# States of the recurrence handed to attention layer 0 in halves of four sequences, and a different order for one stretch of the norms

## The chip, the cores and the metric

The kernel runs on one core of a Trainium2 chip. The metric is device time in microseconds (us) for one execution. Five engines work side by side, each through its own queue in order: TensorE (PE, matmuls; its weight loads are listed as PEld), VectorE (DVE), ScalarE (ACT), GpSimd (POOL) and SyncE (SP, which issues nearly all DMAs). An instruction that waits holds up everything behind it on its engine.

## The reference

The input x has 8 sequences of 512 positions with 128 features. Two blocks follow each other.

```
xb = einsum('bsd,ed->sbe', layernorm(x), B)        # block 1
h  = tanh(h @ A.T + xb_t);  y_t = h @ C.T          # 512 steps in sequence, 8 sequences at once
x  = x + layernorm'(y + layernorm(x)) * gamma + beta
z  = layernorm(x)                                  # block 2: six layers
for i in range(6):
    z = attn(shift(z), Wqkv[i], ...) + z           # 16 heads of 64, window of 32, l2-normed q and k, rotary
    z = ffn(shift(z), W1[i], W2[i], ...) + z       # gated gelu, 341 hidden
out = x + z
```

`shift` takes the second half of the features from the position before. A token of layer 0 needs the state h of its own position, and through the window those of the 32 positions before. Nothing in layer 0 needs a later position, so attention of layer 0 can begin on early positions while the recurrence still runs.

## The kernel before

**The order is written out by hand.** The program is recorded in a manual schedule: each engine executes its instructions in the order in which the Python code emits them. There is no planner; what decides is where a call stands in the code.

**Chunks, parts, groups.** The 512 positions are cut into four chunks of 128. Layer 0's attention works on parts (c, h): chunk c, half h, a half being four sequences. The order of parts is (0,0) (0,1) (1,0) (1,1) (2,0) (3,0) (2,1) (3,1) (line 926). Each part makes two groups, one for each four of the eight pairs of heads, so group n belongs to part n // 2. Layers 1 to 5 have 16 groups each as well, 96 in all.

**Slots.** The main loop (line 1085) runs over n, and inside over t = 0..3. One `slot(n, t)` (line 956) mixes the work of four groups: scores and softmax of group n for 128 query rows (`scores`, `turn`, `less_max`, `exps`, `average`, `divide`, `turn_back`), the norms of group n+1 at t = 0 and 1 (`sums`, `solve`, `spread`, `finish`), the projections of group n+2 at t = 2 and 3 (`unit_a` makes `rawa`, `unit_b` makes `rawb`), and the output projection of group n-1 at t = 1 (`project` makes `yo`, then `add`). Five lists `fill[0]` to `fill[4]` hold what `run(0)` to `run(4)` emit between these.

**Norms.** `sums` adds squares on PE (`nsq`, line 430); `solve` makes inverse roots on DVE; `spread` broadcasts them on PE (`bc`, line 465), one PSUM bank for each of four units; `finish(c)` multiplies unit c with its `bc` on DVE (line 565) and sends it to qT or kbuf by four DMAs. Groups with n < 9 (`NREC`) have a pool of three PSUM banks for `rawa`, `rawb`, `nsq`, `bc`, `vps`, `yo`; later ones have four. In `slot(n, 1)` with n < 9, `spread` is emitted for units 0, 1, 2, then `finish(0)`, `less_max`, `spread` for unit 3, `exps`, `mask`, `finish(1)`, `average`, `finish(2)`, `finish(3)`, `project`, `divide`, `add`.

**Steps of the recurrence.** `Recurrence.step` (line 262) is one matmul `xb` of 128x8 on PE (line 281; two records, since fp32 goes in two passes) and one tanh `hT` on ACT (line 289); the next step's matmul waits for that tanh. Steps enter the stream in two ways. `tick(us)` is called after pieces of PE work with an estimate of their length and emits a step when 0.35 us have gathered. `alone()` (line 356) emits a step and two `warm` matmuls (line 361) that write nothing of use. The first chunk's 128 steps run by `alone()` before any group.

**From states to tokens.** After step 127 of a chunk, `queue(c)` (line 315) makes a list of 21 pieces: two `output` (PE: `yp`, line 302; DVE adds, line 311), the norm of all eight sequences (four `stats` pieces of two sequences, one `rsqrt` of 11 small DVE instructions, two `normalise` of four sequences), two `scale`, one `add` with a store of x1, the second norm in the same form, and two `turn` (PE transposes `rt_c`, ACT copies into xT). `output` sets `held` while steps may not go on. `run(k)` pops one piece at a time, in slots with t = 1 only outside `run(4)` and none that needs a PSUM bank except at `run(0)`.

**Who waits.** `begin(n)` calls `rec.need(c)` (line 377) before the first group of a part on chunk c. It emits `alone()` until the chunk is over and then all 21 pieces in one go, until both halves are posted. Ahead of the first group the loop of lines 1077 to 1081 pops the first chunk's pieces with an `alone()` after each from the third on. `need` is called at the head of a slot, so everything that the slot emits stands behind it on every engine.

Of the kernel before, what the change touches and what calls it, by code (L numbers as in the profile page):

```python
# [48 lines left out]
def mk_seq_preln_kernel(  # L49
# [102 lines left out]
    with tc.tile_pool(name="qk", bufs=2) as qkp, tc.tile_pool(  # L152
# [16 lines left out]
        class Recurrence:  # L169
# [19 lines left out]
            def stats(self, src, nm, bs=range(B)):  # L189
                if bs[0] == 0:  # L190
# [7 lines left out]
            def rsqrt(self, nm):  # L198
                x_, y, a = (
                    small.tile([P, B], F32, tag=f"r{i}", name=f"{i}_{nm}", bufs=1)  # L200
                    for i in "xya"
                )
                nc.vector.tensor_scalar_add(x_, self.mv[:, :, 1], EPS)
# [7 lines left out]
                self.rs = y  # L211
# [103 lines left out]
            def queue(self, c):  # L315
# [9 lines left out]
                def add():  # L325
                    nc.vector.tensor_add(x1, x1, o)
                    nc.sync.dma_start(x1_d[:, c], x1)

                def turn(q):
                    tp = self.turned(o, f"c{c}", q)  # L330
                    sq = slice(4 * q, 4 * q + 4)
                    nc.scalar.copy(xT[:, sq, c * P : (c + 1) * P], tp)
                    nc.scalar.copy(self.edge[D // 2 :, sq, c], tp[D // 2 :, :, P - 1])
                    if q:
                        self.posted = c + 1

                def norm(dst, src, nm):
                    for b in range(0, B, 2):
                        yield lambda b=b: self.stats(src, nm, (b, b + 1)), False
                    yield lambda: self.rsqrt(nm), False  # L340
                    for b in range(0, B, 4):
                        yield lambda b=b: self.normalise(dst, src, range(b, b + 4)), False


                self.pieces = [(lambda q=q: self.output(c, o, q), True) for q in range(2)]
                self.pieces += norm(o, o, f"b{c}")
                self.pieces += [(lambda: scale(slice(0, 4)), False)]
                self.pieces += [(lambda: scale(slice(4, 8)), False), (add, False)]
                self.pieces += norm(o, x1, f"c{c}")
                self.pieces += [(lambda q=q: turn(q), True) for q in range(2)]  # L350

# [25 lines left out]
            def need(self, c):  # L377

                while self.posted <= c:
                    if self.pieces:  # L380
                        self.piece()
                    else:
                        self.alone()
# [36 lines left out]
        class Norms:  # L420
# [3 lines left out]
            def __init__(self, sqs, which, op, floor, nm, inside):  # L424

                nsq = mm(f"nsq_{nm}")
                for half in range(len(sqs[0])):
# [10 lines left out]
                    rec.tick(0.93)  # L438
# [496 lines left out]
        def begin(n):  # L935
# [3 lines left out]
            if l == 0:  # L939
                c, h = b  # L940
                if g == 0:
                    rec.need(c)
# [13 lines left out]
        def slot(n, t, feed=None):  # L956
# [10 lines left out]
            back, bt = (cur, t - 2) if t > 1 else (old, NT - 2 + t)  # L967
            fill = [[] for _ in range(5)]
# [9 lines left out]
            if one and t == 1:  # L978
                fill[1] = [lambda: one.spread(range(4)), lambda: one.finish(0)]
                if n < NREC:  # L980

                    fill[1] = [lambda: one.spread((0, 1, 2)), lambda: one.finish(0)]
                    fill[2] = [lambda: one.spread((3,))]
# [36 lines left out]
            if feed and t == 2:  # L1020
                feed.apply()
            if cur:
# [12 lines left out]
            if one and t == 1:  # L1035
                one.finish(1)
            if last:
                last.average(lt)
            if one and t == 1 and not feed:
# [20 lines left out]
        with tc.manual_schedule():  # L1060
# [16 lines left out]
            for _ in range(2):  # L1077
                rec.piece()
            while rec.posted == 0:
                rec.piece()  # L1080
                rec.alone()
# [3 lines left out]
            for n in range(-1, len(todo) + 1):  # L1085
                m, l = n % GL, n // GL
                if n == NREC:
                    rec.need(NT - 1)
# [144 lines left out]
```

## Time and profile before

| | us |
|---|---|
| median of 3 runs (lowest, highest) | 3875.51 (3870.49, 3880.85) |
| profiled execution | 3878.7 |
| its span, first to last instruction | 3876.6 |
| first step of the recurrence to the last | 19.6 to 598.4 |
| scores of group 9, t = 0 (the first without the recurrence's pool) | 660.2 |

All that the change touches lies in the first 660 us of the span. "Busy" is the time in which an engine has an instruction running; the granted clock of PE is 1.00 at full speed and 0.50 at half. A row of the timeline gives the start, the duration of the rows merged in it, engine, line, operation and tile, and in brackets how long the engine was idle ahead of it and what it waited for.

Start of the scores (line 627) of each slot in us, read from PE's timeline:

| n | t=0 | t=1 | t=2 | t=3 |
|---|---|---|---|---|
| 0 | 176.6 | 183.5 | 193.6 | 202.7 |
| 1 | 214.1 | 223.2 | 238.9 | 246.8 |
| 2 | 292.6 | 301.8 | 317.5 | 325.4 |
| 3 | 336.8 | 345.9 | 361.6 | 370.4 |
| 4 | 381.7 | 391.0 | 406.6 | 414.6 |
| 5 | 425.9 | 438.8 | 456.8 | 469.2 |
| 6 | 496.6 | 505.8 | 521.6 | 529.5 |
| 7 | 541.7 | 550.9 | 566.6 | 574.5 |
| 8 | 625.8 | 632.2 | 644.9 | 651.1 |
| 9 | 660.2 | 667.0 | 675.8 | 682.2 |

### The profile page before, as it was taken

What the parts mean: (1) busy time and instruction counts of PE and PEld (TensorE: products, weight loads), DVE (VectorE), ACT (ScalarE), POOL (GpSimd) and SP (SyncE); (2) the same over time, 40 slices, a digit from 0 to 9 for tenths busy, and PEclk for the clock granted to TensorE, in tenths of its full rate; (3) what the DMA queues carried; (4) which work ended last, traced back from release to release, by engine and by line L of the source; (5) the groups of instructions that cost most, each with busy time, mean ns of one, the idle gap of its engine ahead of it and who ended that gap; (6) DMA issues with size and microseconds to landing.
All of it is one profiled execution on the core that took longest, in us unless ns stands there. A gap on an engine that the chain in (4) does not pass through costs nothing.

```text
span 3876.6 us, 159331 instructions
## 1 busy us (share of the span) xinstructions
PE 3553.3 (92%) x70178; PEld 2141.7 (55%) x70180; DVE 2542.5 (66%) x5208; ACT 1932.1 (50%) x3864; POOL 1827.0 (47%) x780
## 2 busy tenths in 40 slices
PE   8879897899999999999999999999999999999997
PEld 4556664545555555555555555555555555555553
DVE  3555655767677677677677677677677677677673
ACT  2344443545455455455455455455455455455452
POOL 0333332536365365355355355355355355365450
PEclk9889888999999999999999999999999999999998
DMA  3233443545345355355255354355354355354342
GB/s 124 64 82 86 97 100 86 121 94 128 77 111 116 69 125 126 77 115 114 67 127 125 74 117 113 72 128 120 73 117 110 75 130 120 77 117 111 73 110 60
DMA packets 366078, 390.54 MB, mean 101 GB/s; under 512 B 96846, under 2 KB 262220, under 8 KB 365260
## 3 DMA queue, kind: packets, MB, share of 16 engines
q1 hardware_dynamic: 364380, 378.09, 42.7%
q8 instruction: 553, 9.06, 1.1%
q10 hardware_dynamic: 1008, 2.27, 0.2%
q14 instruction: 137, 1.12, 0.1%
HBM read 34.56 MB, written 14.20 MB: 13 GB/s over the span
## 4 chain that ended last, share of the span: by engine, by line
PE 67%; DVE 20%; ACT 7%; issue 4%; DMA 1%; SPq 0%; DVEq 0%; ACTq 0%
PE sc L627 6%; PE rawb L538 5%; PE vps L587 5%; PE tp L656 4%; PE yo L712 4%; PE rawa L526 4%; DVE t L565 4%; PE nsq L430 4%; PE at L703 3%; PE fa L883 3%; DVE t L516 3%; PE xb L281 3%; PE yf L909 3%; PE fg L887 3%; DVE e L643 3%
## 5 line engine op out<-in xcount | busy, mean ns | idle before, releaser
L548 POOL TENSOR_TENSOR u<-rope_sb,bs 128x1024 f32<-128x1024 f32 x320 | 767.5, 2398 | 1349.7 <-ACT bs L544 1171.9
L549 POOL TENSOR_TENSOR t<-t,u 128x1024 f32<-128x1024 f32 x320 | 756.5, 2364 | 25.1
L565 DVE TENSOR_TENSOR t<-t,bc 128x1024 f32<-128x1024 f32 x320 | 376.1, 1213 | 287.2 <-PE bc L465 287.1
L516 DVE SCALAR_TENSOR_TENSOR t<-rawa,par_sb,rope_sb 128x1024 f32<-128x1024 f32 x320 | 409.4, 1279 | 204.4 <-ACT sq L530 199.0
L650 ACT ACTIVATE e<-e 128x512 f32<-128x512 f32 x320 | 201.8, 631 | 433.2 <-DVE e L643 319.4
L661 ACT COPY eT<-tp 128x512 f32<-128x512 f32 x320 | 187.4, 586 | 452.6 <-PE tp L656 452.6
L627 PEld LDWEIGHTS sc<-kbuf,qT 64*32 64x32 f32 x20480 | 226.5, 105 | 257.0 <-ACT sc L617 161.5
L627 PE MATMUL sc<-kbuf,qT 64*32 64x64 f32 x20480 | 280.1, 225 | 85.1 <-ACT sc L617 83.9
L538 PE MATMUL rawb<-xbuf,wqk 128*128 128x512 f32 x640 | 344.0, 619 | 0.0
L587 PE MATMUL vps<-wv,xbuf 128*64 128x256 f32 x2560 | 331.4, 391 | 0.0
L526 PE MATMUL rawa<-xbuf,wqk 128*128 128x512 f32 x640 | 328.3, 594 | 1.7 <-DVE t L516 1.7
L712 PE MATMUL yo<-aoT,wo 128*128 128x512 f32 x640 | 297.7, 608 | 33.4 <-DVE t L565 32.5
L674 PEld LDWEIGHTS av<-vbuf,eT 64*32 64x32 f32 x20480 | 227.2, 105 | 182.6 <-ACT sq L542 110.7
L674 PE MATMUL av<-vbuf,eT 64*32 64x65 f32 x20480 | 284.4, 225 | 14.5 <-issue 11.2
L692 DVE TENSOR_TENSOR ao<-av,rc 128x256 f32<-128x256 f32 x640 | 271.4, 424 | 21.9
L530 ACT ACTIVATE sq<-rawa 128x512 f32<-128x512 f32 x320 | 190.1, 594 | 153.5 <-PE rawa L526 153.5
L281 PEld LDWEIGHTS xb<-hT,s1w 128*128 128x128 f32 x1022 | 169.4, 198 | 174.2 <-ACT hT L289 118.4
L656 PE MATMUL tp<-ident,e 128*128 128x128 f32 x1280 | 205.9, 283 | 43.1 <-DVE rc L691 42.5
L587 PEld LDWEIGHTS vps<-wv,xbuf 128*64 128x64 f32 x2560 | 162.9, 137 | 140.1 <-issue 66.8
L643 DVE TENSOR_TENSOR e<-sc,mx 128x512 f32<-128x512 f32 x320 | 221.3, 692 | 27.5 <-PE rawa L526 0.5
L289 ACT ACTIVATE hT<-xb 128x8 f32<-128x8 f32 x512 | 91.5, 179 | 293.9 <-PE xb L281 279.6
L617 ACT CAST sc<-mask_sb 128x512 f32<-128x512 bf16 x384 | 227.7, 593 | 0.0
(282 smaller groups left out, 6264.3 us busy)
## 6 DMA issues: line engine op xcount, KB each, us to landing
qT<-t SPq DMA_DIRECT2D x640, 128.0 KB
kbuf<-t SPq DMA_DIRECT2D x640, 128.0 KB
vbuf<-vbuf SPq DMA_DIRECT2D x544, 130.0 KB
vbuf<-vbuf SPq DMA_DIRECT2D x160, 97.5 KB
xbuf<-xT SPq DMA_DIRECT2D x95, 128.0 KB
xbuf<-xT SPq DMA_DIRECT2D x80, 127.8 KB
wqk<-in_w_qkv SPq DMA_DIRECT2D x12, 512.0 KB
xf<-xT SPq DMA_DIRECT2D x24, 256.0 KB
```

What stands on the lines that cost most here:

```text
L516: nc.vector.scalar_tensor_tensor(t, self.twice(raw), scale, self.rope(isk, 1), ALU.mult, ALU.mult)
L526: nc.tensor.matmul(raw, self.wqk[:, c, 0], self.xs[:, WINDOW:], start=True, stop=True)
L538: nc.tensor.matmul(raw, self.wqk[:, c, 1], self.xs[:, WINDOW:], start=True, stop=True)
L548: nc.gpsimd.tensor_mul(self.wide(u), self.rope(isk, 0), self.twice(bs))
L549: nc.gpsimd.tensor_add(self.ts[c], self.ts[c], u)
L565: nc.vector.tensor_mul(t, t, self.bcs[c].unsqueeze(1).to_broadcast([P, 2, S]))
L587: nc.tensor.matmul(ps[par * KB : (par + 1) * KB, j], self.xs[:, k0 : k0 + KB], self.wv[:, par * GP * DH : (par + 1) * GP * DH], start=True ...
L627: nc.tensor.matmul(self.sc[blk * QB : (blk + 1) * QB, par, i, :], self.qT[rows, i, q0 : q0 + QB], kT[rows, i, :], start=False, stop=True, ...
L643: nc.vector.tensor_sub(self.e.rearrange("p i a k -> p a i k"), self.sc, mx.unsqueeze(3).to_broadcast([P, 2, GP, KB]),)
L656: nc.tensor.transpose(tp[:, i, :], self.e[:, i].rearrange("p a k -> p (a k)"), ident)
L674: nc.tensor.matmul(av[blk * QB : (blk + 1) * QB, i, :VW], self.eT[rows, i, blk * QB : (blk + 1) * QB], self.v[rows, BT * t + blk, i, :], s ...
L712: nc.tensor.matmul(self.yp, wo[:, self.g * GP + c, :], self.aoT[:, c, :], start=(c == 0), stop=(c == GP - 1),)
```

## The change

It has four parts, all in the phase of the recurrence.

1. `queue` makes 24 pieces instead of 21: both `output`, then for each half its own first norm (two `stats`, one `rsqrt` over four sequences, one `normalise`), `scale`, `add` with a store of half of x1, second norm and `turn`. `posted` counts halves, and `need(c, h)` waits for half h alone.
2. While `need` pops pieces it now emits one `alone()` step after each, unless steps are held or over.
3. `Norms` calls `tick` four times over its matmuls where it was called twice.
4. In `slot(n, 1)` with n < 9, `spread` is emitted for units 0 and 1 with `finish(0)` and `finish(1)` ahead of `less_max`, and for units 2 and 3 in `run(4)`, behind `project` and `divide` and ahead of `add`, with `finish(2)` and `finish(3)`; `average` moves ahead of `less_max`.

```diff
+            def rsqrt(self, nm, bs=slice(0, B)):
...
-                def add():
-                    nc.vector.tensor_add(x1, x1, o)
-                    nc.sync.dma_start(x1_d[:, c], x1)
+                def add(bs):
+                    nc.vector.tensor_add(x1[:, bs], x1[:, bs], o[:, bs])
+                    nc.sync.dma_start(x1_d[:, c, bs], x1[:, bs])
...
-                    if q:
-                        self.posted = c + 1
+                    self.posted = 2 * c + q + 1
...
+                self.pieces += [(lambda q=q: self.output(c, o, q), True) for q in range(2)]
+                for q in range(2):
+                    bs = slice(4 * q, 4 * q + 4)
+                    self.pieces += norm(o, o, f"b{c}{q}", bs)
+                    self.pieces += [(lambda bs=bs: scale(bs), False)]
+                    self.pieces += [(lambda bs=bs: add(bs), False)]
+                    self.pieces += norm(o, x1, f"c{c}{q}", bs)
+                    self.pieces += [(lambda q=q: turn(q), True)]
...
-            def need(self, c):
-
-                while self.posted <= c:
-                    if self.pieces:
-                        self.piece()
-                    else:
+            def need(self, c, h):
+
+                while self.posted <= 2 * c + h:
+                    self.piece()
+                    if self.t < S and not self.held:
                         self.alone()
...
-                    rec.tick(0.93)
+                        if m % 2:
+                            rec.tick(0.47)
...
-                    rec.need(c)
+                    rec.need(c, h)
...
+            tight = n < NREC
...
-                if n < NREC:
-
-                    fill[1] = [lambda: one.spread((0, 1, 2)), lambda: one.finish(0)]
-                    fill[2] = [lambda: one.spread((3,))]
+                if tight:
+                    fill[1] = [lambda: one.spread((0, 1)), lambda: one.finish(0)]
+                    fill[1] += [lambda: one.finish(1)]
+                    fill[4] = [lambda: one.spread((2, 3)), lambda: one.finish(2)]
+                    fill[4] += [lambda: one.finish(3)]
...
+            if tight and t == 1 and last:
+                last.average(lt)
             if cur:
                 cur.less_max(t)
...
-            if one and t == 1:
+            if one and t == 1 and not tight:
                 one.finish(1)
-            if last:
+            if last and not (tight and t == 1):
                 last.average(lt)
-            if one and t == 1 and not feed:
+            if one and t == 1 and not feed and not tight:
                 one.finish(2)
                 one.finish(3)
```

More of the change, by code (lines that the diff above doesn't have):

```diff
@@ L189, in stats @@
             def stats(self, src, nm, bs=range(B)):
-                if bs[0] == 0:
+                if bs[0] == 0 or bs[0] == 4 and len(bs) == 2:
                     self.mv = small.tile([P, B, 2], F32, tag="mv", name=f"mv_{nm}", bufs=1)
@@ L196, in stats @@
                     nc.vector.bn_aggr(mv[:, b, :], st)
[L198 to L201, printed above, removed]
+            def rsqrt(self, nm, bs=slice(0, B)):
+                self.rs = small.tile([P, B], F32, tag="ry", name=f"y_{nm}", bufs=1)
+                y = self.rs[:, bs]
+                x_, a = (
+                    small.tile([P, B], F32, tag=f"r{i}", name=f"{i}_{nm}", bufs=1)[:, bs]
+                    for i in "xa"
                 )
-                nc.vector.tensor_scalar_add(x_, self.mv[:, :, 1], EPS)
+                nc.vector.tensor_scalar_add(x_, self.mv[:, bs, 1], EPS)
                 nc.vector.tensor_scalar(
@@ L210, in rsqrt @@
                     nc.vector.scalar_tensor_tensor(y, a, 1.5, y, ALU.add, ALU.mult)
-                self.rs = y
             def normalise(self, dst, src, bs=range(B)):
@@ L333, in turn, with norm @@
                     nc.scalar.copy(self.edge[D // 2 :, sq, c], tp[D // 2 :, :, P - 1])
-                    if q:
-                        self.posted = c + 1
-                def norm(dst, src, nm):
-                    for b in range(0, B, 2):
+                    self.posted = 2 * c + q + 1
+                def norm(dst, src, nm, bs):
+                    for b in range(bs.start, bs.stop, 2):
                         yield lambda b=b: self.stats(src, nm, (b, b + 1)), False
[L340 to L350, printed above, removed]
+                    yield lambda: self.rsqrt(nm, bs), False
+                    yield lambda: self.normalise(dst, src, range(bs.start, bs.stop)), False
+                self.pieces += [(lambda q=q: self.output(c, o, q), True) for q in range(2)]
[6 more added lines that the diff above has]
+                    self.pieces += [(lambda q=q: turn(q), True)]
             def piece(self, bank=True):
@@ L1076, in mk_seq_preln_kernel @@
                 rec.alone()
[L1077 to L1081, printed above, removed]
+            rec.need(0, 0)
             for t in (2, 3):
@@ L1087, in mk_seq_preln_kernel @@
                 if n == NREC:
-                    rec.need(NT - 1)
+                    rec.need(NT - 1, 1)
                     recs.close()
```

## The prediction, made before the changed kernel ran

> **What bounds the kernel now.** I read the page's first lines, then the waits of PE in the phase of the recurrence, then PE, ACT and DVE over one slot, then stretches with their granted clock.
>
> ```profile
> span 3876.6 us, 159331 instructions
> PE 3553.3 (92%) x70178; PEld 2141.7 (55%) x70180; DVE 2542.5 (66%) x5208; ACT 1932.1 (50%) x3864; POOL 1827.0 (47%) x780
> ```
>
> PE is the bound. From group 9 on (660 us) the changed program keeps every engine's order, so only the first 660 us can move. PE's waits from 130 to 660 us (total, times, longest):
>
> ```profile
> PE rt_c L228 <- issue: 36.4, 2, 18.2
> PE xb L281 <- ACT hT L289: 11.0, 12, 5.4
> ...
> PE bc_c1h L465 <- DVE t_c1h L565: 4.2, 4, 1.1
> PE bc_c0h L465 <- DVE t_c0h L565: 4.0, 4, 1.1
> ```
>
> Two waits of 18.2 us are the flushes of all pieces for chunks 1 and 3. The `bc` waits are `spread(3)`, which needs the bank that `finish(0)` frees. What such a short wait costs is seen in slot (3,1), PE:
>
> ```profile
> 348.35 1.17 PE L465 MATMUL bc_c1h<-k_c1h,selt_sb 32*128 32x128 f32 x24
> 349.45 0.39 PE L281 MATMUL xb<-hT,s1w 128*128 128x8 f32 x2
> 350.89 1.35 PE L465 MATMUL bc_c1h<-k_c1h,selt_sb 32*128 32x128 f32 x8 [1.05 <-DVE t_c1h L565]
> ...
> 353.74 2.06 PE L712 MATMUL yo_c0h<-aoT_c0h,wo 128*128 128x512 f32 x2
> ...
> 359.34 1.10 PE L712 MATMUL yo_c0h<-aoT_c0h,wo 128*128 128x512 f32 x2
> 360.43 1.10 PE L526 MATMUL rawa_c1h<-xbuf,wqk 128*128 128x512 f32 x2
> ```
>
> The same `yo` takes 2.06 and then 1.10. The granted clock says why (stretch: length, PE busy, clock, DMA share, GB/s):
>
> ```profile
> 349.49:350.89 1.40, 0.35 (x6) 1.00 0.05 12
> 350.89:351.86 0.97, 0.97 (x8) 0.93 0.00 0
> 351.86:358.66 6.80, 6.80 (x77) 0.51 0.84 188
> ```
>
> An idle of 1.05 us is followed by 6.8 us at half clock, a loss of 3.4 us; together 4.45. This happens in all eight slots (0,1) to (7,1). In (8,1), without steps, an idle of 1.37 us brought only about 3.4 us at half. The Trainium skill ("TensorE: Matmul & The Clock Gate", section "HAM oscillation — how this bites in real kernels") tells one to avoid PE gaps above about 3.4 us. By that rule gaps of 1 to 2 us cost only themselves. The rows above disagree, and they decide. ACT and DVE in the same slot:
>
> ```profile
> 352.25 0.63 ACT L650 ACTIVATE e_c0h<-e_c0h 128x512 f32<-128x512 f32 x1 [2.20 <-DVE e_c0h L643]
> 352.79 0.58 ACT L617 CAST sc<-mask_sb 128x512 f32<-128x512 bf16 x1
> 353.92 0.18 ACT L289 ACTIVATE hT<-xb 128x8 f32<-128x8 f32 x1 [0.55 <-PE xb L281]
> ```
>
> ```profile
> 349.61 1.22 DVE L565 TENSOR_TENSOR t_c1h<-t_c1h,bc_c1h 128x1024 f32<-128x1024 f32 x1 [4.75 <-PE bc_c1h L465]
> 350.75 0.68 DVE L640 TENSOR_REDUCE mx_c0h<-sc 128x8 f32<-128x512 f32 x1
> 351.47 0.69 DVE L643 TENSOR_TENSOR e_c0h<-sc,mx_c0h 128x512 f32<-128x512 f32 x1
> ```
>
> A tanh stands behind `exps` and `mask` on ACT, and these wait for DVE. Now the late `bc` hides that: the tanh is asked for at 353.9, after `mask` is done.
>
> **The change, part by part.** Counts of steps and pieces come from following the loops of both versions.
>
> (a) *First chunk.* The chain of pieces on DVE for eight sequences runs from 110.9 to 130.1; the transposes start at 128.44. For four: stats 8 rows in 1.6, `rsqrt` 2.3 (11 rows at 0.20; it does not shrink), `normalise` 1.1, `scale` 1.3, `add` 0.65, stats 1.6, `rsqrt` 2.3, and 0.45 into the last `normalise`: transposes at 122.3, a gain of 6.1. The transfer to xbuf behind them (2.4 us, awaited in both) moves with them, so the first `rawa` gains the same. The 11 pieces of the second half now stand between `unit_a` and `unit_b` of slots (-2,2) and (-2,3): on DVE 6.3 us in the first of these, delaying the third unit's DVE product and with it the bank for the fourth `rawb` by 4 to 6, then 7 us ahead of `solve`; plus a `turn` of 1.1. I take +8. Sum **+2**; ends -6 (second half hidden) and +7 (13.3 for it, half of the 26.6 of (c), less the gain).
>
> (b) *Chunk 1, slot (2,0).* Ten steps alone instead of 12 at 0.66 each: -1.3. Transposes 6.1 earlier, as in (a), and four instead of eight ahead of `nsq`: -1.1. The 12 steps beside the pieces cost nothing: PE idled there. The second half is spread over (2,0) to (2,2), where POOL has just been idle and DVE has no backlog: 0.8 for a late accumulator bank, 0.8 for `less_max`, `turn` 1.1, 1.0 for late unit products: +3.7. Sum **-4.8**; ends -8.5 and +4.8 (13.3 for the half).
>
> (c) *Chunk 2.* Group 5 took 70.7 us (425.9 to 496.6) where its neighbours took 44.1, so its spread pieces cost 26.6, among them `yp` 4.0 and a last forced flush. DVE pieces beside POOL are slow at times: four `normalise` rows took
>
> ```profile
> 461.16 3.20 DVE L215 TENSOR_SCALAR o<-o,mv_b,y_b 128x128 f32<-128x128 f32 x4
> ...
> 466.99 1.11 DVE L215 TENSOR_SCALAR o<-o,mv_b,y_b 128x128 f32<-128x128 f32 x4
> ```
>
> Afterwards the steps are over at (4,2), the pieces lie evenly up to (5,3), and nothing is flushed. There are two more `rsqrt` (4.4 on DVE). I follow DVE: `yp` 4.0; in (5,0) `less_max` comes 5 to 8 late and a step's tanh behind it, and the half `turn` waits, together 7.7; (5,1) 2.3; (5,2) 1.5; (5,3) 3.5; half clock 1.5. That is 20.5, so **-6**; ends -13 (half of the cost gone) and +4.4 (the added `rsqrt` alone).
>
> (d) *Chunk 3.* Before, slot (7,3) to (8,0) took 51.2: 9.0 of slot, 23 steps alone 15.1, `yp` to transposes 22.3, transposes 2.2, `nsq` 2.7. Afterwards the steps end in (7,3): slot without eight steps 7.4, `yp` 4.0, nine pieces flushed with PE idle 11.0, transposes 1.1, `nsq` 2.7: 26.2, a gain of 25. Slots (8,0) to (8,3) took 34.4 and get the other half without steps to hide it: DVE has 6.5 of its own in (8,0) and gets 6.3 more; then `rsqrt` stands ahead of `finish(2)` in (8,1). I count 44.3, +9.9. Sum **-15**; ends -25 and -8 (17 instead of 9.9, 1.3 times the half's 13.3).
>
> (e) *More steps at ticks.* Two per `sums` and one per `spread`, each 0.26 to 0.32 on PE between small matmuls (one between two `nsq` runs: 146.81 to 147.13), taken 0.31, for eight groups: 24 x 0.31 = **+7.4**; ends 6 and 8. They are what lets the 23 lone steps go.
>
> (f) *Slots (n,1).* Time from the scores, rows of (3,1): two `bc` units 0.73 instead of 1.10, step, `average`, so the first `yo` starts at 4.5, the second ends at 6.7 at full clock. DVE now does two `finish` (from 3.4, 1.135 apart) before `less_max`: `exps` at 7.2, `mask` 7.7, and the tanh of `project`'s first step only at 8.2 to 8.4. `project`'s second step needs it: PE idles 6.7 to 8.45, **1.75 us**. Moving `average` up puts its own tanh ahead of `exps`, one step too few. Then `bc` for units 2 and 3, and the next `rawa` takes the bank that `finish(2)` frees: the old wait, **1.05**, at a new place. Behind it on PE stand the scores of t = 2. Full-clock work is 14.5 - 4.45 + 0.3 = 10.35 up to `rawa`, so 13.1 with both idles, against 14.5. Half clock set in 0.1 to 1.4 us after such an idle and lasted 6.8; the second idle lies in or right behind that, so I expect 6.8 to 12 us at half, 3.2 to 5.9 lost, partly in t = 2. Per slot +1.8 to +4.5, taken +3.1. Seven slots 21.7, and (0,1), with no `project`, +2: **+24**. Ends: -36 (8 x 4.45, both idles covered after all) and +36. By the skill's rule, with no clock loss on either side, it would be 13.1 - 11.1, +14 for seven.
>
> At no cost: eight DMAs of `finish(2)` and `finish(3)` leave some 10 us later on SP, with nothing awaited behind them, and kbuf is read two slots (19 us) later; a transfer took 4.0. Four more stores of x1 wait on DVE adds that are earlier anyway. `add` after `finish(3)` frees a bank for the third unit only, 4 us later.
>
> **Sum:** 2 - 4.8 - 6 - 15 + 7.4 + 24 = +7.6 on the profiled execution's 3878.7: 3886.3. The median, 3875.5, is 3.2 lower: **3883**.
>
> **Rivals.**
> 1. *Ends on the other side: spreading does hide.* If the idles of (f) lose the clock no more often than now, (f) is 0 and the sum is -16: 3859. With the waits really gone, -36 and -52: 3823. It decides where the tanh of `project` isn't behind `exps`; for: DVE idles 4.75 us before `finish(0)`; against: the order on ACT.
> 2. *DVE becomes the bound wherever halves are spread.* Each spread half costs its full 13.3 in (a), (b), (d): +5.3, +9.6, +3.4, and (f) at its upper end +12: sum +38, 3913. For: group 5's 26.6; against: POOL idle in (2,0).
> 3. *Halving does little* because `rsqrt` doesn't shrink and freed flushes come back as stalls: (a), (b), (c) at 0, (d) -8, (e) +7.4, (f) 0: -0.6, 3875.
>
> **How the numbers follow.** Forecast 0.5 (own range 3871 to 3898), rival 1 0.25, rival 2 0.15, rival 3 0.10. About 0.3% (11.6 us) is what a measurement of this kernel tells from no change. From the forecast: slower 0.24, same 0.22, faster 0.04; rival 1 faster; rival 2 slower; rival 3 mostly same. With ends from rivals 1 and 2: 3846 to 3912.
>
> **What would show it.** Right: transposes 16 us behind `yp` instead of 22; no flush above 12 us; no warm matmul after slot (2,0); in slots (n,1) no wait at `bc` in `spread`, a wait of `xb` on `hT` near 1.75 and of `rawa` on `t` near 1.05, `rawa` at 2.06. Wrong: full clock through (n,1), or group 5 above 70 us.

## The result, and the profile after

The changed kernel takes 3916.26 us (median; 3906.68 to 3923.41) against 3875.88, a ratio of 1.0103 (95% interval 1.0076 to 1.0129). It is slower by about 40. Its profiled execution took 3913.45, 34.8 more than that of before. The page's first lines:

```profile
span 3911.7 us, 159335 instructions
...
PE 3576.4 (91%) x70139; PEld 2159.5 (55%) x70140; DVE 2578.4 (66%) x5300; ACT 1932.7 (49%) x3864; POOL 1825.5 (47%) x780
```

The page counts 39 PE instructions fewer than before (39 rows of `warm`, which write nothing of use) and 23.1 us more of busy time: no more work, but at a lower clock. By group 9 (scores of t = 0 at 697.7 instead of 660.2) all of the loss is there. Where it arose (scores of t = 0 to scores of t = 0), beside what the prediction's terms come to there, (e) and (f) included:

| stretch | before | after | difference | predicted |
|---|---|---|---|---|
| start to scores of (0,0) | 176.6 | 198.1 | +21.5 | +2.9 |
| (0,0) to (2,0) | 116.0 | 111.9 | -4.1 | -1.6 |
| (2,0) to (3,0) | 44.2 | 55.7 | +11.5 | +7.7 |
| group 3 | 44.9 | 46.6 | +1.7 | +4.0 |
| groups 4, 5 | 114.9 | 129.0 | +14.1 | +2.0 |
| group 6 | 45.1 | 48.2 | +3.1 | +4.0 |
| (7,0) to (8,0) | 84.1 | 65.3 | -18.8 | -21 |
| (8,0) to (9,0) | 34.4 | 42.9 | +8.5 | +9.9 |

The waits of PE from 120 to 720 us (total, times, longest), in the same view as before:

```profile
PE rt_c L229 <- issue: 23.8, 3, 15.1
PE rt_c L229 <- DVE o L216: 23.0, 2, 15.0
PE xb L282 <- ACT hT L290: 10.1, 13, 1.7
PE tp_c1h L656 <- DVE rc_c1h L691: 4.3, 2, 4.0
```

Two flushes of 18.2 have become 15.1 and 4.3. But there are new waits: 15.0 for the transposes of chunk 0's second half, 8.0 for those of chunk 2 (5.1 before), and 4.0 for DVE's reciprocals in slot (5,0). (Line numbers of the changed kernel differ by up to two.)

The waits alone do not make the 37.5: up to group 9 PE's idle time grew by 10.5 (91.5 to 102.0) and its busy time by 27.0 (568.7 to 595.7). The granted clock makes most of it. Read in stretches of half a microsecond from 120 to 720, PE was busy at half clock for 96.1 before and 162.9 after; half of the difference is 33.4, and shorter work takes some of that back. Three stretches of 34 us each hold 85.5 of the 162.9: 147.5 to 181.5, 301 to 335.5 and 468.5 to 502.5; before, none held more than 10.1 of busy time, and the longest without an idle was 7.0. One of them (stretch: length, PE busy, clock, DMA share, GB/s):

```profile
297.00:300.00 3.00, 0.49 (x4) 1.00 0.23 87
300.00:303.00 3.00, 1.17 (x6) 0.69 0.00 0
303.00:306.00 3.00, 3.00 (x35) 0.50 0.32 64
306.00:312.00 6.00, 6.00 (x118) 0.50 0.07 15
312.00:324.00 12.00, 12.00 (x110) 0.50 0.08 18
324.00:333.00 9.00, 9.00 (x168) 0.50 0.34 83
333.00:336.00 3.00, 3.00 (x8) 0.62 0.72 160
```

The flush of slot (2,0) ends with 4.3 of idle. Then PE is busy without a gap for 33 us, and stays at half. The full clock came back while the 512-column `yo` of slot (2,1) ran.

**Why the second turn waited 15.0.** Right after the rows of `rope` on POOL begin, DVE has the second half's `rsqrt`. DVE, POOL and PE in slots (-2,3) to (-1,0):

```profile
136.39 2.29 DVE L205 TENSOR_SCALAR x_b<-mv_b 128x4 f32<-128x4 f32 x1
138.71 2.31 DVE L206 TENSOR_SCALAR y_b<-x_b 128x4 int32<-128x4 int32 x1
141.06 0.16 DVE L210 SCALAR_TENSOR_TENSOR a_b<-x_b,y_b 128x4 f32<-128x4 f32 x1
141.25 2.21 DVE L211 TENSOR_TENSOR a_b<-a_b,y_b 128x4 f32<-128x4 f32 x1
143.50 2.33 DVE L212 SCALAR_TENSOR_TENSOR y_b<-a_b,y_b 128x4 f32<-128x4 f32 x1
145.86 0.16 DVE L210 SCALAR_TENSOR_TENSOR a_b<-x_b,y_b 128x4 f32<-128x4 f32 x1
```

```profile
136.31 2.35 POOL L549 TENSOR_TENSOR t_c0h<-t_c0h,u_c0h 128x1024 f32<-128x1024 f32 x1
138.62 2.38 POOL L548 TENSOR_TENSOR u_c0h<-rope_sb,bs_c0h 128x1024 f32<-128x1024 f32 x1
141.07 2.37 POOL L549 TENSOR_TENSOR t_c0h<-t_c0h,u_c0h 128x1024 f32<-128x1024 f32 x1
143.41 2.41 POOL L548 TENSOR_TENSOR u_c0h<-rope_sb,bs_c0h 128x1024 f32<-128x1024 f32 x1
```

```profile
160.53 1.25 PE L229 MATMUL rt_c<-ident,o 128*128 128x128 f32 x4 [14.99 <-DVE o L216]
161.71 1.12 PE L587 MATMUL vps_c0h<-wv,xbuf 128*64 128x256 f32 x4
162.76 0.60 PE L282 MATMUL xb<-hT,s1w 128*128 128x8 f32 x2
163.29 1.12 PE L587 MATMUL vps_c0h<-wv,xbuf 128*64 128x256 f32 x4
```

A row of four elements a partition takes 0.16 when POOL is idle, and otherwise until the POOL instruction beside it is over. Then `turn` stands on PE ahead of `values`, waits, and the products behind it run at half clock (1.12 instead of 0.65).

**Slot (3,1), PE**, which the prediction had worked out in steps:

```profile
381.75 1.10 PE L712 MATMUL yo_c0h<-aoT_c0h,wo 128*128 128x512 f32 x2
384.53 0.39 PE L282 MATMUL xb<-hT,s1w 128*128 128x8 f32 x2 [1.67 <-ACT hT L290]
384.77 1.10 PE L712 MATMUL yo_c0h<-aoT_c0h,wo 128*128 128x512 f32 x2
...
387.01 1.16 PE L465 MATMUL bc_c1h<-k_c1h,selt_sb 32*128 32x128 f32 x16
388.10 0.39 PE L282 MATMUL xb<-hT,s1w 128*128 128x8 f32 x2
389.55 1.77 PE L526 MATMUL rawa_c1h<-xbuf,wqk 128*128 128x512 f32 x2 [1.06 <-DVE t_c1h L565]
```

Both new waits are there in the sizes forecast (1.67 for 1.75, 1.06 for 1.05). Behind the first the clock stayed full this time, behind the second it was half for 3.5.

### The profile page after: what moved, and what is told of

Its sections match the earlier page's. It is cut to its first block, busy times and chain, and to the rows that moved or that the text cites. A ratio compares the mean times of both kernels' runs of the same rounds, so it can differ in the third digit from the quotient of the medians.

```text
span 3911.7 us, 159335 instructions
## 1 busy us (share of the span) xinstructions
PE 3576.4 (91%) x70139; PEld 2159.5 (55%) x70140; DVE 2578.4 (66%) x5300; ACT 1932.7 (49%) x3864; POOL 1825.5 (47%) x780
## 4 chain that ended last, share of the span: by engine, by line
PE 69%; DVE 18%; ACT 7%; issue 3%; DMA 2%; SPq 0%; ACTq 0%; DVEq 0%
PE sc L627 6%; PE rawb L538 5%; PE yo L712 5%; PE vps L587 5%; PE rawa L526 5%; PE tp L656 5%; PE nsq L429 4%; PE at L703 4%; DVE t L565 3%; PE fa L883 3%; PE xb L282 3%; PE yf L909 3%; PE fg L887 3%; DVE t L516 3%; PE av L674 2%
## 5 line engine op out<-in xcount | busy, mean ns | idle before, releaser
L712 PE MATMUL yo<-aoT,wo 128*128 128x512 f32 x640 | 297.8, 608 | 35.5 <-DVE t L565 34.7
L674 PEld LDWEIGHTS av<-vbuf,eT 64*32 64x32 f32 x20480 | 226.7, 105 | 181.2 <-ACT sq L542 110.7
L674 PE MATMUL av<-vbuf,eT 64*32 64x65 f32 x20480 | 283.0, 225 | 14.0 <-issue 10.5
L282 PEld LDWEIGHTS xb<-hT,s1w 128*128 128x128 f32 x1022 | 179.1, 210 | 180.4 <-ACT hT L290 113.2
```

Source lines behind the costliest of these rows:

```text
L282: nc.tensor.matmul(self.xb[:, k, :], abc[:, 0, :], self.hT[:, (t - 1) % P, :], start=False, stop=True, skip_group_check=True,)
L674: nc.tensor.matmul(av[blk * QB : (blk + 1) * QB, i, :VW], self.eT[rows, i, blk * QB : (blk + 1) * QB], self.v[rows, BT * t + blk, i, :], s ...
L712: nc.tensor.matmul(self.yp, wo[:, self.g * GP + c, :], self.aoT[:, c, :], start=(c == 0), stop=(c == GP - 1),)
```

## The experiments

The theory after the result: **(A)** DVE's short pieces are blocked by POOL's products, the work behind them waits, and the idle costs PE its clock for as long as the following work is short matmuls with steps between. Its rival is the prediction's second: **(B)** a spread half costs some 13 of DVE time wherever it stands. Ratios are to the kernel before, run on the same chip. From group 9 on all kernels execute the same order, and yet that rest took 3209 to 3223 in their profiles. So positions are compared by the start of group 9 (one profile each), times by ratio.

| run | ratio to before (95%) | group 9 at |
|---|---|---|
| before | 1 | 660.2 |
| the change | 1.0103 (1.0076 to 1.0129) | 697.7 |
| 1 start_whole | 1.0047 (1.0032 to 1.0061) | 680.1 |
| 2 no_rope_g0 | 1.0071 (1.0056 to 1.0086) | 687.0 |
| 3 dense_20 | 1.0088 (1.0060 to 1.0116) | 685.3 |
| 4 burst | 1.0091 (1.0066 to 1.0117) | 691.7 |
| 5 gate | 0.9991 (0.9980 to 1.0002) | 661.4 |
| 6 gate_dense_old | 0.9980 (0.9968 to 0.9992) | 655.8 |
| 7 part4_undone | 1.0066 (1.0041 to 1.0091) | 681.7 |
| 8 need_ticks | 0.9953 (0.9938 to 0.9968) | 641.1 |
| 9 need_ticks_part4 | 1.0007 (0.9990 to 1.0023) | 658.6 |
| 10 need_ticks_gate | 0.9987 (0.9974 to 1.0001) | 647.5 |
| 11 need_ticks_late | 0.9975 (0.9964 to 0.9985) | 645.8 |
| 12 need_ticks_late_gate | 0.9949 (0.9934 to 0.9963) | 637.4 |
| 13 late_gate_part4 | 0.9955 (0.9940 to 0.9971) | 639.5 |
| 14 late_gate_halves | 1.0000 (0.9989 to 1.0010) | 661.6 |
| 15 halves_where_they_pay | 0.9947 (0.9934 to 0.9961) | 638.4 |

### 1 and 2: the start

start_whole:

```diff
-            rec.need(0, 0)
+            rec.need(0, 1)
```

> The changed kernel, but ahead of the first group both halves of chunk 0 are drained, as before. Theory A (the 11 spread pieces of the second half run beside GpSimd's rope products, so that single DVE rows of 0.16 take 2.2 to 2.3, PE waits 15.0 for the second turn and then stays at half clock up to 181.5): scores of slot (0,0) go back from 198.1 to 178 to 180, no wait of rt_c above 2 there, time -18 to -20 against the changed kernel: 3896 to 3898. Theory B (a spread half costs 13.3 of DVE time wherever it is put, no clock and no GpSimd in it): 13.3 comes back, the earlier start of 6.1 is lost: -7, 3909.

Scores of (0,0) came at 181.2 and the time fell by 0.56%, some 22, within about 12 either way. That is A's size (18 to 20) rather than B's 7. Draining both halves with PE idle is cheaper here than hiding one.

no_rope_g0:

```diff
+                if self.n == 0:
+                    return
                 u = tmp.tile([P, 2, S], F32, tag="u", name=f"u_{nm}")
                 nc.gpsimd.tensor_mul(self.wide(u), self.rope(isk, 0), self.twice(bs))
                 nc.gpsimd.tensor_add(self.ts[c], self.ts[c], u)
```

> The changed kernel without GpSimd's two rope products for group 0 (eight instructions of 2.4; group 0's q and k keep only the first of their two rope terms). Theory A (GpSimd's products block DVE's short rows): the rows of the second half's two rsqrt in slots (-2,2) to (-1,0) take 0.16 to 0.20 each instead of up to 2.33, the second turn comes 11 to 12 earlier, PE waits 3 to 4 for it instead of 15.0; what half clock follows may stay, so -11 to -20 against the changed kernel: 3896 to 3905. Theory B (the rows are slow for a reason of their own, or wait for something else): they stay at 2.2, and the time moves by less than 3.

The same DVE rows without POOL beside them, and the second turn on PE:

```profile
136.54 0.16 DVE L205 TENSOR_SCALAR x_b<-mv_b 128x4 f32<-128x4 f32 x1
136.73 0.17 DVE L206 TENSOR_SCALAR y_b<-x_b 128x4 int32<-128x4 int32 x1
136.94 0.16 DVE L210 SCALAR_TENSOR_TENSOR a_b<-x_b,y_b 128x4 f32<-128x4 f32 x1
137.13 0.16 DVE L211 TENSOR_TENSOR a_b<-a_b,y_b 128x4 f32<-128x4 f32 x1
```

```profile
148.87 1.25 PE L229 MATMUL rt_c<-ident,o 128*128 128x128 f32 x4 [3.18 <-DVE o L216]
150.04 1.12 PE L589 MATMUL vps_c0h<-wv,xbuf 128*64 128x256 f32 x4
```

The rows start 0.15 later than in the changed kernel and take 0.16 instead of 2.29. The wait is 3.18 instead of 14.99. Scores of (0,0) came 11.0 earlier, and the time fell by 0.32% (12, within about 12). So the rows show the block. The half clock behind the shorter wait stayed (148 to 172), as A allowed.

The Trainium skill ("SBUF — State Buffer", section "Who interferes with whom") has this as a rule: VectorE and GpSimd share one pair of ports. An operation with two inputs in SBUF contends for it with a GpSimd instruction that reads SBUF; so does one in a two-port mode, which a scalar operation can enter, and there whoever comes second is blocked for the whole instruction. The rows agree: 2.2 to 2.3 beside POOL rows of 2.35 to 2.41. The statistics, with one SBUF input, kept 0.26 to 0.28 beside POOL (rows 153.68 to 154.6 of the changed kernel).

### 3 and 4: the clock behind an idle

dense_20:

```diff
                     if self.t < S and not self.held:
                         self.alone()
+                        if c == 1:
+                            self.warm("b")   # the two idle matmuls of alone(), once more
```

> The changed kernel, with one more pair of idle matmuls behind each step that is run while pieces are popped at the head of slot (2,0); they write nothing of use and lie beside the chain of pieces on DVE, on which PE waited 4.34 at its end. Theory A (the long half-clock stretch 301 to 335.5 comes from that idle, and lasts because the short matmuls with steps between that follow cannot raise the clock): the stretch is gone, half of its 33.7 busy us comes back, -14 to -17 against the changed kernel: 3899 to 3902, although PE executes more. Theory B (the idle costs itself and at most one spell of 6.8 at half clock, as the prediction priced such idles; the chain on DVE sets the end of slot (2,0) anyway): 0 to -3.4, 3913 to 3916; and if the added matmuls delay the transposes, up to +4.

```profile
304.48 1.05 PE L229 MATMUL rt_c<-ident,o 128*128 128x128 f32 x4 [2.68 <-issue]
305.37 0.33 PE L282 MATMUL xb<-hT,s1w 128*128 128x8 f32 x2
305.55 0.80 PE L365 MATMUL warm<-mask_sb,ident_b 128*128 128x512 bf16 x2
306.14 0.85 PE L365 MATMUL warm_268b<-mask_sb,ident_b 128*128 128x512 bf16 x2
306.92 1.08 PE L435 MATMUL nsq_c0h<-sq_c0h,sel_sb 128*32 128x128 f32 x16
...
309.53 0.64 PE L435 MATMUL nsq_c0h<-sq_c0h,sel_sb 128*32 128x128 f32 x16
```

The idle of 2.68 again took the clock, but only from 305.5 to 309, instead of 34.5 us. Slots (2,0) to (3,0) took 46.0 instead of 55.7 in the profiles: -9.7. The times do not resolve it: the ratio fell by 0.15%, which is 6 within about 15. A expected 14 to 17. Part of what is missing came back as another wait: at full clock PE is at the `xb` of slot (2,1) earlier, and waits 2.46 instead of 0.70 for the tanh behind `exps`.

burst:

```diff
                 ps = pst.rearrange("p (j c) -> p j c", j=2)
+                for _ in range(8 if k == 0 and self.n in (0, 3, 6) else 0):
+                    nc.tensor.matmul(pst, ident_b, mask_sb.rearrange("p a i k -> p (a i k)")[:, :S], ...)
```

> The changed kernel with eight idle matmuls of 128x512 ahead of the first product of values in slots (-1,0), (2,0) and (5,0), 24 in all, 1.7 us each time at full clock and 3.4 at half; they write into a bank that the product then overwrites. All three waits stay as they are. Theory A (after an idle the clock stays at half as long as only short matmuls with a step between follow, and a dense run of 3.4 or more brings it back): the three half-clock stretches end 3 to 7 us behind the bursts instead of at 181.5, 335.5 and 502.5; about 12, 15 and 24 us of half clock go, half of which is gained, less 10 for the bursts: -12 to -18, 3898 to 3904. Theory B (all three lasted 34 us, so the time is fixed once the clock has dropped): the stretches end where they did and the bursts cost 3.4 each: +10, 3926.

```profile
160.06 1.24 PE L229 MATMUL rt_c<-ident,o 128*128 128x128 f32 x4 [14.69 <-DVE o L216]
161.53 3.19 PE L585 MATMUL vps_c0h<-mask_sb,ident_b 128*128 128x512 bf16 x7 [0.22 <-issue]
164.65 0.67 PE L596 MATMUL vps_c0h<-wv,xbuf 128*64 128x256 f32 x4
```

The first stretch ended at 164.5 instead of 181.5, right behind the burst: 34 us is no fixed time, so theory B of this run falls. But the gain that A expected did not come. Group 9 began 6.0 earlier, and the median of the times, 3920.06, is not below the changed kernel's. Half-clock work fell from 162.9 to 110.5; the bursts cost 3.2 in slot (-1,0) and 1.9 in slot (2,0), and PE's idle time up to group 9 grew by 9.3 (102.0 to 111.3). The second stretch ended at 311.5 as its burst began, behind nothing but short matmuls and steps. The third ended at 468.5, inside its burst (465.9 to 468.9), but one of 17 us began at 485.5, in a wait of 2.46. So two of three stretches ended with a burst. That short work keeps the clock at half is likely, not certain.

### 5 and 6: pieces kept from POOL

gate:

```diff
-                    yield lambda: self.rsqrt(nm, bs), False
+                    yield lambda: self.rsqrt(nm, bs), False, True      # likewise normalise, scale, add
...
+                port = t == 1 or t == 0 and k >= 2 or t == 2 and k < 2
-                    rec.piece()
+                    rec.piece(True, port)     # a piece with True as third entry waits for port
```

> The changed kernel, but the pieces that GpSimd's products block on DVE (both rsqrt, normalise, scale, add) are popped only where GpSimd is idle: in slots (n,1), in the second half of slots (n,0) and at the first two places of slots (n,2); the statistics, whose rows kept 0.26 to 0.28 beside GpSimd, go anywhere. Theory A (block and clock): the rsqrt rows are back at 0.16 to 0.17, the wait of 15.0 at the second turn of chunk 0 and the one of 3.95 in slot (5,0) go, and with them the half-clock stretches 147.5 to 181.5 and 468.5 to 502.5; -17 at the start, as in the run with chunk 0 drained whole, and -15 in groups 4 and 5: 3884 (3878 to 3895). The stretch behind slot (2,0) stays. Theory B (a spread half costs its 13.3 on DVE wherever it is put): -3 to +3, since as many pieces are spread.

1.0103 became 0.9991: -43, within about 11, with the halves spread as before, only at other places, and as many instructions. Groups 4 and 5 took 103.9 instead of 129.0. This is A, and more than it expected (32). The stretch behind slot (2,0) stayed (288 to 325.5).

gate_dense_old puts `gate`, the added matmuls of `dense_20` (in every drain) and the old order of slots (n,1) together:

```diff
+                        self.warm("b")
+                    elif self.t == S:
+                        for k in range(4):
+                            self.warm(f"_{len(self.pieces)}_{k}")
...
-            tight = n < NREC
+            tight = False
```

> The changed kernel with the pieces kept from GpSimd's products as in the run before, idle matmuls behind the steps and pieces that are popped at the head of slots (in all of them, four pairs a piece once the steps are over), and the norms of slots (n,1) in the old order. Theory A: the gains add up, -32 for the pieces, -9 for slot (2,0) as measured with added matmuls there, -3 for slot (8,0), -2 to -13 for the order: 3860 to 3870, below the kernel before. Theory B (clock and waits come back elsewhere): above 3885.

0.9980: the sum of the parts did not come; group 9 began 5.6 earlier than in `gate`, where 14 or more were expected. The profile says why. The same two added matmuls behind the same idle (2.69) did not bring the clock back this time: it was half from 293 to 334. In `dense_20` the clock fell 0.98 behind the start of the first transpose, here 0.88 (worked out from the mean clock of stretches of 1 us, 0.73 and 0.95). A tenth of a microsecond between the program and the moments at which the clock changes went with 3.5 or 41 us of half clock. That it was the cause is not shown: the two programs differ ahead of this place.

### 7, 9 and 13: part 4, three times

part4_undone (the changed kernel, norms of slots (n,1) in the old order):

```diff
-            tight = n < NREC
+            tight = False
...
+                if n < NREC:
+                    fill[1] = [lambda: one.spread((0, 1, 2)), lambda: one.finish(0)]
+                    fill[2] = [lambda: one.spread((3,))]
```

> The changed kernel with the norms of slots (n,1) back in the old order (three units broadcast at once, the fourth behind less_max, average behind finish(1)); halves, ticks and need stay. Prediction's term (f): the new order costs 24, so -24 against the changed kernel: 3892. Trace of the changed kernel: groups 3 take 46.6 against 44.9 before, of which the ticks alone explain 0.9, and slot (3,1) took 15.7 in both kernels, so the new order costs about 0.7 a group, 5 in all: -5 to 0, 3911 to 3916. Rival 1 of the prediction (the new order is a gain of 36 that is hidden by other losses): +36, 3952.

need_ticks_part4 (run 8 below with part 4 added):

```diff
+            tight = n < NREC
...
+                    fill[1] = [lambda: one.spread((0, 1)), lambda: one.finish(0)]
+                    fill[1] += [lambda: one.finish(1)]
+                    fill[4] = [lambda: one.spread((2, 3)), lambda: one.finish(2)]
+                    fill[4] += [lambda: one.finish(3)]
```

> The kernel before with parts 2, 3 and 4 of the change, norms whole: against the run with parts 2 and 3 alone (3862.6) this prices part 4 by itself. Prediction's term (f): +24, 3887. If the 13 that the changed kernel gained when part 4 was undone are the order's own cost: 3876. If they are the order's cost only together with spread halves (slots (5,0) to (5,3), 17.6 of the 16 there), as the equal length of group 3 in both says (46.7 and 46.6): 0 to +5, 3863 to 3868.

Undoing part 4 gave 0.37% (14, within about 14); adding it to whole norms cost 0.54% (21, within about 9). Both are nearer to the prediction's 24 than to the 0 to 5 that was read from group 3, though the first alone would hardly tell them apart. But the slots put it elsewhere: groups 1 to 3 together took 163.8 without and 165.4 with part 4 (runs 8 and 9), groups 4 and 5 took 111.3 and 125.2. Most of that difference begins with one wait in slot (4,3). DVE, ACT and PE of run 9:

```profile
424.21 2.33 DVE L204 TENSOR_SCALAR y_b<-x_b 128x8 int32<-128x8 int32 x1
426.57 0.17 DVE L208 SCALAR_TENSOR_TENSOR a_b<-x_b,y_b 128x8 f32<-128x8 f32 x1
426.77 2.19 DVE L209 TENSOR_TENSOR a_b<-a_b,y_b 128x8 f32<-128x8 f32 x1
...
430.28 0.68 DVE L640 TENSOR_REDUCE mx_c1h<-sc 128x8 f32<-128x512 f32 x1
```

```profile
431.86 0.63 ACT L650 ACTIVATE e_c1h<-e_c1h 128x512 f32<-128x512 f32 x1 [7.41 <-DVE e_c1h L643]
432.39 0.58 ACT L617 CAST sc<-mask_sb 128x512 f32<-128x512 bf16 x1
432.91 0.16 ACT L289 ACTIVATE hT<-xb 128x8 f32<-128x8 f32 x1
```

```profile
433.12 0.59 PE L281 MATMUL xb<-hT,s1w 128*128 128x8 f32 x2 [7.35 <-ACT hT L289]
```

Part 4 lets one step more into each slot (n,1), ten for nine, so chunk 2 is over earlier in slot (4,2), five of its pieces are popped there instead of four, and every later piece stands one place earlier. `rsqrt` now stands ahead of `less_max` on DVE, beside POOL. `exps` waits for `less_max`, a tanh waits behind `exps` on ACT, and PE's next step waits 7.35 for it. The clock was half from 430.5 to 488.5. (Run 8 waited 4.16 for reciprocals in slot (5,0), and half clock lasted from 438 to 468.5.)

late_gate_part4 adds the same lines to run 12, where no blocked piece stands there:

> The kernel before with parts 2, 3 and 4, late begins and the pieces kept from GpSimd: against the same without part 4 (3855.0) it prices part 4 where no piece is blocked ahead of less_max. If part 4 costs 13 to 14 by itself, as two runs had it: 3869. If those came from a piece moved by one place (the wait of 7.35 in slot (4,3) and the 58 us of half clock behind it), and groups 1 to 3 show its own cost (163.8 against 165.4 for three groups): +0.5 a group, 3855 to 3860.

0.9955 against 0.9949: +2, within about 8 either way. So the order of part 4 costs little by itself. The 21 of run 9 came from a piece that it displaced, and more from the clock behind it than from the wait.

In the changed kernel the path was not the same. There a blocked `rsqrt` stands behind `less_max`, and PE waits for the reciprocals behind it, once 3.95:

```profile
461.66 2.20 DVE L210 SCALAR_TENSOR_TENSOR a_b<-x_b,y_b 128x4 f32<-128x4 f32 x1
...
471.47 1.09 PE L656 MATMUL tp_c1h<-ident,e_c1h 128*128 128x128 f32 x4 [3.95 <-DVE rc_c1h L691]
```

With part 4 undone another `rsqrt` is blocked in the same way, and the wait is longer:

```profile
505.12 2.27 DVE L206 TENSOR_SCALAR y_b<-x_b 128x4 int32<-128x4 int32 x1
...
511.88 1.09 PE L656 MATMUL tp_c1h<-ident,e_c1h 128*128 128x128 f32 x4 [7.43 <-DVE rc_c1h L691]
```

In groups 4 and 5 PE idled for 16.5 with part 4 and 15.3 without, but it was busy at half clock for 54.4 and 21.8. Half of that difference is 16.3 of the 17.6 between them. So what part 4 cost the changed kernel there is clock, not waiting. Why 34 us of half clock went with the wait of 3.95 and 7 with that of 7.43 is not settled.

### 8: parts 2 and 3 alone

```diff
-                    if self.pieces:
-                        self.piece()
-                    else:
+                    self.piece()
+                    if self.t < S and not self.held:
                         self.alone()
...
-                    rec.tick(0.93)
+                        if m % 2:
+                            rec.tick(0.47)
...
```

Ahead of the first group, `need(0)` takes the place of the old loop that popped the first chunk's pieces, as `need(0, 0)` does in the change.

> The kernel before with parts 2 and 3 of the change alone: steps run while pieces are popped at the head of a slot, and twice as many places for a step in the sums; norms whole over eight sequences, old order in slots (n,1). Prediction's terms: (e) +7.4; the 23 lone steps of slot (8,0) 15.1 go, four of the pieces move into slot (7,3) -4; the forced flush at slot (6,0) goes -6; slot (2,0) -1.3: 3875.5 - 19 = 3857. Theory with the clock: the flush of 18.2 idle at slot (2,0) gets 13 steps that do not reach its end, so the half-clock spell behind it stays short, because eight transposes and the sums without steps between are dense: the same -19. Rival (the halves carry the gain of the change and the steps at ticks are the loss): 3875 to 3883.

0.9953 (0.9938 to 0.9968), -18, and group 9 19.1 earlier, where 19 were forecast. From slot (7,3) to (8,0) it took 35.5 instead of 51.3: most of what the change gains at chunk 3 is that steps are over by then. The halves add 5.4 (30.1) and take back 9.9 in slots (8,0) to (9,0) (33.0 against 42.9).

### 10 to 12: two ways to spread whole norms

need_ticks_gate is run 8 with the lines of `gate`; need_ticks_late begins a part later:

```diff
-                if t == 1 or n + 2 not in groups:
+                due = t > 1 or todo[n + 2][0] or rec.posted > todo[n + 2][1][0]
+                if due and (t == 1 or n + 2 not in groups):
                     begin(n + 2)
```

> The kernel before with parts 2 and 3, and the pieces that GpSimd blocks kept to places where GpSimd is idle. Theory (block and clock): the half-clock stretch of 30.5 in chunk 2's spread (438 to 468.5, 27.4 busy, 13.7 lost) goes, but the second rsqrt, two normalise and both turns come due at slot (6,0), an idle of about 5: -8, 3855. Rival: what is kept back is paid in full at slot (6,0) with its clock: 3863 to 3868.

> The kernel before with parts 2 and 3, and the first group of a part begins only at t = 2 of a slot where its chunk is not yet posted, instead of at t = 0, since its projections stand there; so pieces of chunks 1 and 3 are spread over two more slots before what is left is drained. Theory: of 21 pieces some 9 to 13 are then done beside other work; the idle of 19.4 ahead of slot (8,0) falls by about 10, the drain in slot (2,0) by as much, less 3 each for the transfer to xbuf that is then awaited: -14, 3849. Rival (spread pieces come beside GpSimd and the short idles cost clock): 3860 to 3870.

> Both of the runs before together, since slots (2,0), (2,1), (8,0) and (8,1) are where GpSimd is mostly idle: if both theories hold, -22, 3841; if only one of them, the better of the two.

Neither alone gained: 0.9987 and 0.9975, both above run 8. With `gate`, pieces that came due at slot (6,0) were waited for (6.5 at `rt_c`) and half clock followed (479.5 to 500). With late begins, 34 us of half clock came in chunk 2 (477.5 to 511.5). Both rivals held there. Together they gave 0.9949 (-20): late begins give the gated pieces room, no stretch at half clock held more than 8.2 of busy time, and their sum was 75.2 against 95.5 in run 8. The expected 3841 was not reached; run 12's median is 3854.99, and its ratio cannot be told from run 8's 0.9953.

### 14 and 15: halves with the obstacles out of the way

late_gate_halves is `gate` with late begins, old order in slots (n,1), and two steps behind each drained piece:

```diff
-                    if self.t < S and not self.held:
-                        self.alone()
+                    for _ in range(2):
+                        if self.t < S and not self.held:
+                            self.alone()
```

> The changed kernel without part 4, with late begins, the pieces kept from GpSimd and two steps instead of one behind each piece that is popped at the head of a slot: halves where neither GpSimd's products nor an early begin is in the way; against the whole norms in the same setting (3855.0). If halves gain where a drain is awaited: the 13 pieces drained in slot (2,2) become 6 and the 14 in slot (8,2) become 15, chunk 0 starts 6 earlier, chunk 2 is late for nothing: -10, 3845. If halves cost their two more rsqrt a chunk wherever they are put (2.3 each, eight of them, on DVE) and the steps come to their end later: +5 to +15, 3860 to 3870.

1.0000: halves lost, by more than expected. Against run 12, (0,0) came 11.4 later and the way to (1,3) took 10.7 longer (half clock 243 to 260). From (1,3) to (8,3) halves then gained 19.8 (359.0 against 378.8). But the recurrence ended so late that no piece of chunk 3 was spread: 15 were drained in slot (8,2), and the nine of the second half ahead of group 9 (31.0 from (8,3) to (9,0), against 9.1).

halves_where_they_pay mends three places. Its expectation had read the slots of run 14 one too far (a row of scores, split by a wait of 4.2, was counted twice). Its 367.0 runs from (1,2) to (8,3), where run 12 took 386.8, so the gain is again 19.8; the drain that it puts ahead of slot (9,1) stands ahead of (9,0).

```diff
-            rec.need(0, 0)
+            rec.need(0, 1)
...
-                    for _ in range(2):
+                    for _ in range(2 if c or len(self.pieces) % 2 else 1):
...
-                port = t == 1 or t == 0 and k >= 2 or t == 2 and k < 2
+                port = rec.t == S or t == 1 or t == 0 and k >= 2 or t == 2 and k < 2
```

> The kernel of the run before with three places mended: chunk 0 drained whole ahead of the first group (its halves cost 11.4 there), one and a half steps on average behind each of its pieces so that the recurrence ends some 10 steps earlier, and pieces popped anywhere once the steps are over, so that slots (8,2) and (8,3) take the last half instead of a drain of 24 ahead of slot (9,1). If halves gain 20 in chunks 1 to 3, as the slots from (1,3) to (9,0) say (367.0 against 387.9): 3855 - 11 to -20 + 5 for the slower start: 3840 to 3849. Rival (what is gained in the drains comes back in slots (8,2) to (9,0), where GpSimd is busy): 3855 to 3865.

0.9947 (0.9934 to 0.9961), median 3853.75. That is the time of run 12 with whole norms, so the rival is nearer: what halves win in the drains is not seen in the sum. Both beat the kernel before by 0.5%, and the change by 1.5%.

## Why the prediction was wrong

The sign was forecast (slower, the largest of the three chances). The size was +7.6 and is +40, just beyond the upper end of the range; the second rival's 3913 is nearest. Its mechanism, DVE as the bound at 13.3 a half, does not hold: the gate run spread the same halves at other places and took 43 less.

Of the signs that were named, the transposes came 16.3 behind `yp`, no `warm` matmul ran after the head of slot (2,0), and the waits of 1.67 and 1.06 came in slots (n,1). Others failed: a flush of 15.1 stayed at chunk 3, where none above 12 was to be, and group 5 took 75.0, above the 70 that was to show the prediction wrong.

- **(a) +2, with its share of (e) and (f) +2.9, measured +21.5; this is the step that failed most.** The transposes came 16.3 behind `yp` (122.85 after 106.54), as worked out. Parts 2 and 3 alone explain 3.9 of the delay (run 8), and with the first chunk drained whole 4.6 is left of it (run 1). The rest came from the 11 pieces placed in slots (-2,2) and (-2,3), which were costed at the durations of rows with POOL idle. The rows that POOL blocks were in the trace of before: four `normalise` at 3.20 instead of 1.11 were shown, but in (c) alone. And the wait that a late `turn` puts ahead of `values` on PE was left out.
- **(b) -4.8, measured about +6 from (1,3) to (3,0)**, (e) and (f) included. Lone steps and transposes moved as said. What was missing is the half clock of 34.5 behind the remaining idle of 4.3; run 3 priced it at 9.7, in one profile. Before, the same flush ended with eight transposes and 32 products without a step between, and the clock was back 4.3 after its first transpose.
- **(c) -6: right, as far as the halves go.** With part 4 undone groups 4 and 5 took 111.4 against 114.9, where -4.1 with (e) had been worked out. The path was not all as told, though: PE waited 7.43 in slot (5,3) behind a blocked `rsqrt`, so some of the agreement is luck. In the changed kernel they took 129.0, the difference being half clock.
- **(d) -15: right, measured -12.7** from (7,3) to (9,0) (85.7, then 73.0): -21.2 up to (8,0) for -25, +8.5 behind it for +9.9. The flush idled for 15.1 instead of 11.0. Run 8 shows that 15.8 of the 21.2 belong to steps, not to halves.
- **(e) +7.4**: with the lone steps it allows to go, (e) and its gains made -18 for -19 (run 8). The 7.4 was not measured alone.
- **(f) +24: the waits were right, the price was not.** 1.67 and 1.06 came where the prediction put them. By themselves they cost about 2, within about 8 (run 13). What was too large is the clock: 6.8 to 12 us at half had been taken for each slot, and slots (1,1) to (7,1) had 3.4 to 10.2, together 44.4, where they had 47.8 before. In slot (3,1) the next `rawa` started 13.7 behind the scores, at full clock all the way, for 13.1 worked out and 14.5 before; `yo`, `rawa` and `rawb` come next there. The change still lost some 14 by part 4, so 24 was nearly met for a wrong reason. Run 9 shows a path that the prediction did not name: other places for the steps, hence for the pieces, hence a blocked `rsqrt` ahead of `less_max`. In the changed kernel itself the loss lies in the half clock of groups 4 and 5, with blocked rows and waits on both sides.

The rule of the Trainium skill that was weighed ("TensorE: Matmul & The Clock Gate", section "HAM oscillation — how this bites in real kernels": avoid gaps above about 3.4 us) is neither confirmed nor a safe bound here. Gaps of 1.06 and 2.68 took the clock, for 3.5 us; one of 2.69 took it for 41.

## What to carry to other kernels

Work that is hidden on DVE has two durations, one beside POOL and one without; cost it at the one that its place gives, and put what POOL blocks where POOL is idle. What an idle on PE costs beyond itself went with what ran next: ahead of long dense products a few us of clock, ahead of short products with dependent steps between up to 34 here, though not every time. Where a queue of pieces is popped by position, count how a part of the change moves the pieces, not only its own instructions, and measure the parts of a change singly: here parts 2 and 3 gained 18, and parts 1 and 4 lost 58, within about 12, beside them.

## What the runs showed of the hardware

- The granted clock changed only at moments 3.41 us apart. In every trace here, each spell of half or full clock between the first change and the last lasted a whole number of times 3.41 us: 3.41 and 6.83 where 3.5 and 7.0 stand above, 34.13 for the three long stretches of the changed kernel.
- Once at half clock, PE stayed there for 30 to 58 us fourteen times, in the changed kernel and in nine of the runs (41.0 in part4_undone, 58.0 in need_ticks_part4). PE was busy for 21 to 53 us of these, mostly with short products and a step between. In the last 3.4 us of thirteen of them rows of 512 columns ran (`yo`, `rawa`, `rawb`); the other is in no_rope_g0 (506.4 to 540.5). What the clock counts as work is not settled by these runs.
- The outcome can turn on little: the same rows behind an idle of 2.7 had 3.5 and 41 us of half clock in two runs. Executions of one kernel lie far apart as well: 16.8 for the changed kernel (four, 3906.68 to 3923.41), 10.4 for that of before over four and 19.0 over nine.
- DVE rows of 128x4 elements, 0.16 alone, take up to 2.33 beside a POOL product of 128x1024, until that is over; a chain of eleven such rows lost 8.5 to four of them.
